# Hand-over of memory between layer 0, the dilation and layer 1, tile by tile, and another order of batches in layer 1

## The chip, the cores and the metric

One core of one Trainium2 chip runs the whole program. The metric is the device time of one execution in microseconds; lower is better. A kernel is timed in several executions and the median is compared. One more execution, taken with the hardware profiler, gives the trace that the numbers below come from.

## What is computed

The reference is a stack of four graph layers over 16 graphs (B = 16) of 1024 nodes (N = 1024) with 128 features, each layer followed by a residual and a layer norm:

```python
x = _layernorm(x + _L0_gnn_ref(x, adj, ...))      # attention over neighbours, then a gate
x = _layernorm(x + _L1_gnn_ref(x, adj, nodemask, ...))
x = _layernorm(x + _L2_gnn_ref(x, adj, ...))      # attention, then three gates
x = _layernorm(x + _L3_gnn_ref(x, adj, ...))      # two graph convolutions
```

Layer 1 first thins the graph out ("dilation") and then runs three SAGE steps over it, with a batch norm over all graphs between them:

```python
def step(carry, n):                    # lax.scan over the 1024 rows, one after the other
    row = jnp.take(carry, n, axis=0); num = jnp.sum(row)
    sf = jnp.where(num > T_DIL, (num + K_DIL - 1) // K_DIL, 1)
    rm = row & (jnp.cumsum(row) % sf == 0)        # and only where the node is valid
    keep = ~rm
    carry = carry.at[n].set(row & keep)
    carry = carry.at[:, n].set(carry[:, n] & keep)
...
out = (einsum('bij,bjd->bid', adj_d, x) / deg) @ Wr + x @ Wx + b    # _sage, then relu and _bn
```

The thinned adjacency of a graph is the "state" of a batch: 1024 x 1024 values in fp8, 8 KB in each of the 128 partitions, 1 MB in all.

## The kernel before

The whole program is unrolled, and a list scheduler of the compiler fixes the order of instructions on every engine ahead of time. It goes by its own estimate of when each instruction can start: where an engine would be free, it takes the first ready instruction in the order of the source. [...] DMAs are issued by SyncE (SP) and by GpSimd (POOL).

On-chip memory is handed out in pools. A pool that is opened where closed pools lay has to wait for their tiles. A pool may do so in two ways: by default ("pool") the first use of any of its tiles waits until all tiles of the older pools below it are free, the last DMA out of them included; with `reuse_waits="tile"` a tile waits only for the older tiles that it lies on. Layers 2 and 3 have the second form already. A pool lays out its buffers in the order in which the source first names them.

- `Yq` (lines 857 to 862) holds the states of all 16 batches: 64 KB on the left side of SBUF for batches 0 to 7, 64 KB on the right side for batches 8 to 15.
- Layer 0 (lines 867 to 980): for each batch `before` (line 888) loads eight slices of the adjacency (`an`, line 895), makes `ab` and `chk` of them and writes the state `Y[b]` (line 905); `attention` (line 930) runs eight steps of score matmul (line 723), masked maximum (`em`, line 942), exponential and weighted sum (line 953); `after` (line 956) gates, normalises (line 772, with the power on GpSimd at line 744) and stores the batch to `x1_d` (line 977). Three batches are in work at a time: `before` of one, `attention` of the one ahead of it, `after` of the one ahead of that.
- The dilation (lines 990 to 1166) goes in 16 steps: 8 column blocks k times two groups g of 8 batches. `prepare` (line 1016) gathers the counts of a block, `fixed_point` (line 1066) finds the removed entries in six evaluations (line 1082), one after the other, and `removal` (line 1118) takes them out of the state of each batch: row sums (line 1128), `q` (line 1130), `keep` (line 1132), the new state (lines 1133 and 1142). In step i the fixed point of step i runs beside the removals of step i-1 and the preparation of step i+1. The two preparations at the start (line 1159) have nothing beside them. Before these stand the lines 999 to 1008: the check value `nomem`, and `dinv`, the power -1/2 of all degrees, on GpSimd (line 1003), turned and sent to DRAM; it is read in layer 3 only.
- In the last column block the states of batches 8 to 15 also go to DRAM (`dil8_d`, line 1144).
- Layer 1 (lines 1222 to 1454) has three steps over all batches in the order 0 to 15. `first` (line 1337) makes the degrees by a matmul (line 1246), brings them back as a broadcast `rdeg` by three small DMAs, splits x in two float32r parts `hi` and `lo` (lines 1236 and 1237), widens the state to float32r (`a`, lines 1256 and 1258) and multiplies (line 1269); `out` (line 1364) applies the weights, `keep` (line 1393) does the next product. Batches 0 to 7 use their state where it lies. The right side is closed on entry and becomes the pool `l1_wide` for `a` (8 buffers) and for `A8` (4 buffers), into which the states of batches 8 to 15 are loaded back.

[...] Layer 0 uses 0 to 3 for the scores (two buffers of two banks), 4 and 5 for `acc`, 6 and 7 for `ph`/`pt`. The dilation before has the row sums `s` in 0 to 2, `pc` in 3 and 4, `s0` in 5 and 6, `pd` in 7.

## Time and profile before

| what | value |
|---|---|
| median of 8 runs | 3125.91 us (3105.04 to 3132.64) |
| the profiled execution's own time | 3121.4 us |
| its span, first to last instruction | 3119.7 us |
| mean granted TensorE clock | 0.966 |
| busy: TensorE, VectorE, ScalarE, GpSimd | 92%, 75%, 65%, 10% of the span |
| layer 0 | up to about 767 us |
| dilation | about 767 to 1184 us |
| layer 1 | about 1184 to 1900 us; layers 2 and 3 from there to the end |

Times inside the execution are counted from the span's first instruction. In the lines of the timeline the first number is the start, the second the duration, then engine, source line, operation, output and inputs; the bracket at the end says how long the engine was idle before it and what ended this. Every table by windows gives for each stretch its length and the busy time of each engine with the number of instructions.

### The profile page before, as it was taken

To read this page: it belongs to the slowest core of one execution; us is meant where nothing else is said; L and a number is where in the kernel's file an instruction comes from. 1 tells how busy PE (TensorE), PEld (TensorE's weight loads), DVE (VectorE), ACT (ScalarE), POOL (GpSimd) and SP (SyncE) were. 2 spreads that over 40 slices of the span, in tenths; PEclk is the share of its full clock that TensorE was granted. 3 is DMA by queue.
4 is the path that set the end of the run, shared out by engine and by line. 5 is a ranking of instruction groups with operands and counts; after the bars stand their busy time and mean duration, and the time that the engine had idled before them with its cause. 6 is when DMAs were issued, how large, how long until landed. Compare 5 with 4: busy or idle time off the path is not lost.

```text
span 3119.7 us, 43208 instructions
## 1 busy us (share of the span) xinstructions
PE 2857.0 (92%) x15442; PEld 1841.0 (59%) x15442; DVE 2331.4 (75%) x5971; ACT 2016.3 (65%) x3393; POOL 327.1 (10%) x292
## 2 busy tenths in 40 slices
PE   7999999996899998999999987999999999989996
PEld 4455555453566655777788874555555555555554
DVE  7888888886899984666678785766767776666665
ACT  5777777774688875655555534766666666666653
POOL 0000000003000001111122231000010010100000
PEclk9999999997999999999999998999999999999997
DMA  5344334440000006223366792011112211111000
GB/s 169 124 148 149 133 131 142 142 135 29 2 2 2 2 6 226 86 82 122 125 214 227 247 325 107 34 55 54 62 67 66 68 64 54 55 55 54 21 14 22
DMA packets 123216, 297.98 MB, mean 96 GB/s; under 512 B 12656, under 2 KB 64624, under 8 KB 115824
## 3 DMA queue, kind: packets, MB, share of 16 engines
q1 hardware_dynamic: 102384, 211.13, 20.6%
q0 software_dynamic: 20608, 84.00, 7.1%
q8 instruction: 124, 2.03, 0.3%
q14 instruction: 100, 0.82, 0.1%
HBM read 211.04 MB, written 84.02 MB: 95 GB/s over the span
## 4 chain that ended last, share of the span: by engine, by line
PE 57%; DVE 22%; issue 5%; ACT 5%; POOL 4%; DMA 2%; POOLq 0%; SPq 0%; DVEq 0%; ACTq 0%
PE acc L1269 9%; PE ph L1510 7%; PE pmm L723 7%; PE acc L1573 5%; PE acc L953 4%; PE ph L765 4%; PE ph L758 4%; PE ph L1373 3%; PE s L1128 3%; POOL ln_rstd L744 3%; DVE ln_st L777 2%; PE ph L1496 2%; DVE mid L1082 2%; PE acc L1246 1%; DVE keep L1132 1%
## 5 line engine op out<-in xcount | busy, mean ns | idle before, releaser
L723 PE MATMUL pmm<-G,hT 128*128 128x512 f32 x1024 | 504.0, 614 | 6.8 <-DVE mx L942 3.5
L723 PEld LDWEIGHTS pmm<-G,hT 128*128 128x128 f32 x1024 | 183.3, 195 | 179.0 <-issue 135.1
L784 ACT ACTIVATE xn<-xn,ln_nb,ln_rstd 128x128 f32<-128x128 f32 x512 | 209.1, 481 | 121.4 <-DVE ln_nb L782 121.3
L1573 PE MATMUL acc<-em,hs 128*128 128x512 f32 x512 | 247.8, 599 | 22.1 <-DVE hs L1570 20.5
L953 PE MATMUL acc<-em,hs 128*128 128x512 f32 x512 | 253.4, 620 | 11.3 <-DVE hs L950 7.9
L744 POOL TENSOR_TENSOR ln_rstd<-ln_rstd,mhalf 128x8 f32<-128x8 f32 x64 | 117.1, 1829 | 1373.9 <-DVE ln_rstd L741 1075.2
L1269 PE MATMUL acc<-a,lo 128*128 128x512 f32 x768 | 241.1, 398 | 1.9 <-DVE lo L1237 1.9
L1269 PE MATMUL acc<-a,hi 128*128 128x512 f32 x768 | 242.0, 399 | 0.9 <-ACT a L1258 0.7
L1128 PE MATMUL s<-step,carry 128*128 128x512 bf16 (+2 forms) x1088 | 212.8, 309 | 3.5 <-DVE carry L1098 3.2
L1130 ACT ACTIVATE q<-s,negc 128x512 f16<-128x512 f32 x256 | 170.6, 694 | 66.8 <-issue 29.3
L1559 DVE CUSTOM_DVE_ANT_0 em<-pmm,msk 128x1024 f32<-128x1024 f32 x128 | 155.7, 1216 | 57.5 <-PE pmm L723 36.4
L1142 ACT ACTIVATE carry<-pc,negone 128x512 fp8e4<-128x512 f32 x256 | 166.7, 695 | 39.7 <-PE pc L1141 29.7
L939 ACT ACTIVATE msk<-carry,l0nbig 128x1024 bf16<-128x1024 fp8e4 x128 | 145.3, 1141 | 62.4 <-DVE mx L942 47.4
L897 ACT ACTIVATE ab<-an 128x1024 bf16<-128x1024 f32 x128 | 134.6, 1052 | 69.6 <-PE pt L904 42.8
L900 DVE SCALAR_TENSOR_TENSOR chk<-an 128x1024 fp8e4<-128x1024 f32 x128 | 156.1, 1219 | 31.3 <-DMA an<-in_adj 30.2
L942 DVE CUSTOM_DVE_ANT_0 em<-pmm,msk 128x1024 f32<-128x1024 f32 x128 | 155.4, 1214 | 27.1 <-PE acc L953 19.3
L1269 PEld LDWEIGHTS acc<-a,lo 128*128 128x128 f32 x768 | 142.8, 188 | 42.8 <-DVE lo L1237 9.5
L953 PEld LDWEIGHTS acc<-em,hs 128*128 128x128 f32 x512 | 93.6, 196 | 123.0 <-issue 95.5
L1554 ACT ACTIVATE msk<-A,nbig 128x1024 bf16<-128x1024 fp8e4 x128 | 145.5, 1138 | 31.0 <-DVE mx L1559 28.7
L905 DVE TENSOR_SCALAR carry<-pt 128x1024 fp8e4<-128x1024 bf16 x128 | 155.1, 1216 | 13.2 <-PE pt L904 12.6
L1573 PEld LDWEIGHTS acc<-em,hs 128*128 128x128 f32 x512 | 92.6, 190 | 117.5 <-issue 79.8
L1269 PEld LDWEIGHTS acc<-a,hi 128*128 128x128 f32 x768 | 141.6, 188 | 33.8 <-ACT a L1258 1.3
(278 smaller groups left out, 6592.3 us busy)
## 6 DMA issues: line engine op xcount, KB each, us to landing
an<-in_adj SPq DMA_DIRECT2D x128, 512.0 KB, 3.4
adj_d<-carry POOLq DMA_DIRECT2D x16, 1024.0 KB, 4.9
A<-dil_d SPq DMA_DIRECT2D x16, 1024.0 KB, 6.3
rdeg<-rdeg_d SPq DMA_DIRECT2D x32, 512.0 KB, 4.2
ag_d<-ag POOLq DMA_DIRECT2D x32, 512.0 KB, 5.4
ag<-ag_d SPq DMA_DIRECT2D x32, 512.0 KB, 6.2
A<-adj_d SPq DMA_DIRECT2D x16, 1024.0 KB, 4.8
xn<-in_x SPq DMA_DIRECT2D x16, 512.0 KB, 3.8
```

Source lines behind the costliest of these rows:

```text
L723: nc.tensor.matmul(p[:, h * 512:(h + 1) * 512], lhsT, rhs[:, h * 512:(h + 1) * 512], start=True, stop=True)
L744: nc.gpsimd.tensor_tensor(r, r, mhalf[:, :n], op=OP.pow)
L784: nc.scalar.activation(r[:, i, :], r[:, i, :], AF.Identity, scale=rstd[:, i:i + 1], bias=nb[:, i:i + 1])
L900: nc.vector.scalar_tensor_tensor(chk, an, 0.0, an, op0=OP.is_gt, op1=OP.not_equal, accum_out=other[:, c:c + 1], saturate=False)
L953: nc.tensor.matmul(s.acc[:, c], hs, em[:, c], start=(jt == 0), stop=(jt == NT - 1))
L1128: nc.tensor.matmul(s[:, lo or 0:], y, twos if lo is None else step[:, :512 - lo], start=(j == 0), stop=(j == len(terms) - 1))
L1130: nc.scalar.activation(q[:, h * 512:(h + 1) * 512], s, AF.Abs, bias=st.negc[:, i:i + 1])
L1142: nc.scalar.activation(Y[b][:, hb, ks], pc, AF.Relu, bias=negone, saturate=False)
L1269: nc.tensor.matmul(acc, part[:, jt, :], pieces[h * NT // 2 + i][:, j, :], start=(jt == 0 and p == 0), stop=(jt == NT - 1 and p == 1))
L1510: nc.tensor.matmul(p, part[:, jt, :], A[:, jt, c], start=(jt == 0 and i == 0), stop=(jt == NT - 1 and i == 1))
L1559: nc.vector.tensor_tensor_reduce(em, e, msk, 1.0, 0.0, op0=OP.add, op1=OP.max, accum_out=mx)
L1573: nc.tensor.matmul(s.acc[:, c], hs, em[:, c], start=(jt == 0), stop=(jt == NT - 1))
```

## The change

1. All pools of layer 0, of the dilation and of layer 1 get `reuse_waits="tile"`.
2. `an`, `ab`, `chk` and `xT` of layer 0 (17,408 bytes in a partition) move to a pool `early` of their own, which is opened first and so lies lowest.
3. The dilation opens its PSUM pools in another order: `s0` gets banks 0 and 1, `pd` bank 2, `s` banks 3 to 5, `pc` banks 6 and 7.
4. The lines 999 to 1008 (check value, power, transposition, store of `dinv`) move behind the two first preparations.
5. The states of batches 0 to 7 lie on the right side and go to DRAM; those of 8 to 15 lie on the left. Layer 1 takes the batches in the order 8 to 15, 0 to 7, in all three steps.

```diff
-    for ctx_, side in ((carry_ctx, "left"), (carry2_ctx, "right")):
+    for ctx_, side in ((carry2_ctx, "right"), (carry_ctx, "left")):
...
-        wts = ph.enter_context(tc.tile_pool(name="l0_w", bufs=1))
...
+        early = ph.enter_context(tc.tile_pool(name="l0_early", bufs=1, reuse_waits="tile"))
+        wts = ph.enter_context(tc.tile_pool(name="l0_w", bufs=1, reuse_waits="tile"))
+        ps_w = ph.enter_context(tc.tile_pool(name="l0_pw", bufs=2, space=PSUM, reuse_waits="tile"))
+        ps_a = ph.enter_context(tc.tile_pool(name="l0_pa", bufs=1, space=PSUM, reuse_waits="tile"))
+        ps_h = ph.enter_context(tc.tile_pool(name="l0_ph", bufs=2, space=PSUM, reuse_waits="tile"))
...
+        work = ph.enter_context(tc.tile_pool(name="l0_work", bufs=1, reuse_waits="tile"))
+        small = ph.enter_context(tc.tile_pool(name="l0_small", bufs=2, reuse_waits="tile"))
...
-                an = work.tile([P, N], F32, name="an", bufs=2)
+                an = early.tile([P, N], F32, name="an", bufs=2)
...
-                ab = work.tile([P, N], BF16, name="ab", bufs=2)
+                ab = early.tile([P, N], BF16, name="ab", bufs=2)
...
-                chk = work.tile([P, N], FP8, name="chk")
+                chk = early.tile([P, N], FP8, name="chk")
...
-                    xT = work.tile([P, N], F32, name="xT")
+                    xT = early.tile([P, N], F32, name="xT")
...
     with ExitStack() as ph:
...
+        sb = ph.enter_context(tc.tile_pool(name="dl_sb", bufs=2, reuse_waits="tile"))
+        small = ph.enter_context(tc.tile_pool(name="dl_small", bufs=3, reuse_waits="tile"))
+        ps_b = ph.enter_context(tc.tile_pool(name="dl_pb", bufs=2, space=PSUM, reuse_waits="tile"))
+        ps_d = ph.enter_context(tc.tile_pool(name="dl_pd", bufs=1, space=PSUM, reuse_waits="tile"))
+        ps_s = ph.enter_context(tc.tile_pool(name="dl_ps", bufs=3, space=PSUM, reuse_waits="tile"))
+        ps_c = ph.enter_context(tc.tile_pool(name="dl_pc", bufs=2, space=PSUM, reuse_waits="tile"))
...
-            if k == NT - 1 and b >= B // 2:
+            if k == NT - 1 and b < B // 2:
                 nc.gpsimd.dma_start(dil8_d[b], Y[b].bitcast(F32))
...
         for s in steps[:G2]:
             for _ in prepare(*s):
                 pass
+
+        nc.vector.tensor_scalar(mx0, mx0, -1.0e15, None, op0=OP.is_lt)
+        nc.vector.tensor_reduce(nomem, mx0, AX.X, OP.max)
+
+        nc.vector.tensor_scalar(deg, deg, 1.0, 1.0, op0=OP.add, op1=OP.max)
+        nc.gpsimd.tensor_tensor(dinv, deg, mhalf[:, 0:1].to_broadcast([P, BT]), op=OP.pow)
+        pt = ps_s.tile([BT, P], F32, name="pt", tag="s")
+        nc.tensor.transpose(pt, dinv, identf)
+        dt = sb.tile([BT, P], F32, name="dt", bufs=1)
+        nc.vector.tensor_copy(dt, pt)
+        nc.sync.dma_start(dinv_d, dt)
...
-        wts = ph.enter_context(tc.tile_pool(name="l1_w", bufs=1))
-        work = ph.enter_context(tc.tile_pool(name="l1_work", bufs=2))
+        wts = ph.enter_context(tc.tile_pool(name="l1_w", bufs=1, reuse_waits="tile"))
+        work = ph.enter_context(tc.tile_pool(name="l1_work", bufs=2, reuse_waits="tile"))
         carry2_ctx.close()
...
+        small = ph.enter_context(tc.tile_pool(name="l1_small", bufs=2, reuse_waits="tile"))
+        ps_h = ph.enter_context(tc.tile_pool(name="l1_ph", bufs=4, space=PSUM, reuse_waits="tile"))
+        ps_a = ph.enter_context(tc.tile_pool(name="l1_pa", bufs=4, space=PSUM, reuse_waits="tile"))
...
-                    if b >= B // 2:
+                    if b < B // 2:
                         st.A = wide_pool.tile([P, NT, N], FP8, name="A8", bufs=4)
...
+        order = [*range(B // 2, B), *range(B // 2)]
...
-            take_turns([step.load(b) for b in range(1 + lead)])
+            take_turns([step.load(b) for b in order[:1 + lead]])
...
-            outs = [step.out(b) for b in range(B)]
+            outs = [step.out(b) for b in order]
...
-                    streams.append(step.load(i + 1 + lead))
+                    streams.append(step.load(order[i + 1 + lead]))
...
-                    streams.append(step.keep(i - 1 - lag[l]))
+                    streams.append(step.keep(order[i - 1 - lag[l]]))
```

## The prediction

> **What bounds the kernel now.** I read the page first: TensorE is busy for 92% of the span, and its row of forty slices dips at the ninth to tenth and at the fifteenth to sixteenth, the two hand-overs that the change is about. Then the busy times by window around them (length; busy time of each engine; granted clock, DMA share and GB/s at the end):

> ```profile
> 700.00:740.00 40.00, 39.65 (x144) 19.84 (x142) 30.38 (x84) 27.90 (x43) 22.95 (x3) 1.00 0.10 40
> 746.60:767.00 20.40, 7.06 (x88) 6.70 (x88) 6.68 (x26) 4.50 (x10) 2.59 (x2) 0.55 0.09 27
> 767.00:777.20 10.20, 2.66 (x64) 2.50 (x64) 10.20 (x41) 0.00 (x0) 0.00 (x0) 0.50 0.02 7
> 777.20:800.00 22.80, 12.17 (x128) 7.29 (x128) 18.38 (x48) 5.89 (x10) 0.00 (x0) 0.65 0.00 1
> 1164.00:1184.00 20.00, 17.52 (x139) 9.89 (x138) 9.28 (x16) 18.74 (x32) 3.79 (x7) 1.00 0.74 301
> 1184.00:1197.00 13.00, 3.53 (x17) 1.42 (x15) 0.00 (x0) 1.23 (x3) 1.06 (x2) 0.82 0.84 285
> 1197.00:1203.70 6.70, 6.13 (x24) 4.92 (x24) 4.38 (x9) 5.23 (x8) 0.19 (x1) 0.59 0.75 214
> 1203.70:1229.70 26.00, 25.29 (x125) 18.08 (x125) 15.43 (x27) 15.89 (x19) 3.44 (x4) 1.00 0.53 193
> ```

> TensorE, full until 740, does 7.1 us of work in the 20.4 us after the last attention product (746.6) and is cold until 800; VectorE, full from 767 to 777, is idle for two thirds before. In layer 1's first 13 us nearly everything stands still. The chain of waits says what ends the first gap:

> ```profile
> 757.54 1.66 POOL ln_rstd L744
> 759.20 3.70 issue
> 762.92 3.86 DMA x_d<-xn
> 766.90 0.29 DVE dt L1007
> ```

> and the timeline what stands in front of what:

> ```profile
> 711.79 20.75 POOL L1003 TENSOR_TENSOR deg<-deg,mhalf 128x128 f32<-128x128 f32 x1 [0.87 <-DVE deg L1002]
> 735.76 0.17 DVE L782 SCALAR_TENSOR_TENSOR ln_nb<-ln_mv,ln_rstd 128x8 f32<-128x8 f32 x1 [0.45 <-POOL ln_rstd L744]
> 766.90 0.29 DVE L1007 COPY dt<-pt 128x128 f32<-128x128 f32 x1 [7.50 <-DMA x_d<-xn]
> 1183.20 0.33 SPq L702 DMA_DIRECT2D Wr<-in_L_gnn_Wr  x1
> 1188.47 6.62 SPq L1319 DMA_DIRECT2D n<-x_d  x3
> 1196.92 1.05 ACT L1236 CAST hi<-n 128x1024 fp32r<-128x1024 f32 x1 [8.79 <-DMA n<-x_d]
> ```

> `dt` has nothing to do with the store of batch 15, yet waits for it: the pool wait. VectorE then holds all of `prepare` behind it. Layer 1's first load is issued when the last removal ends (1183.2), behind five small loads, among the last stores of states (DMA share 0.84), and lands at 1196.9.

> [...] line 1033 follows 0.2 us after `dt`, though its state was ready at 710. [...] the trace has 3.86 us for 512 KB and that is used.

> **Part by part.**

> *Start.* Now the first `an` is issued at 7.69, after the transposed weights (line 816, 6.96 + 0.28) free the raw pool below `work`. `early` lies on nothing old, so it can go after the six small loads (last 3.14 + 0.47): 3.6. ScalarE starts at 12.61 now. Worth 7.69 - 3.6 = 4.1; VectorE is at constants until 7.4, before the data would land (about 8.5), so little is lost: 3.5 us, between 0 (if `xn`, which still lies on the raw weights, stands ahead on SP) and 4.1. Layer 0 is a full TensorE pipeline, so this moves the rest.

> *Layer 0 to dilation.* By the sizes, `sk` (4096 bytes), `front` (6144), `uY` (1024), `dt` (512), `mid` (2048) and half of `q` lie on `early`, whose last readers end at about 708. `s0` waits for the score bank last used by step 6 of the last attention (739.5), `pd` for step 7 (742.3). What then has to run on VectorE from 742.5 on to the first `keep` (794.9 now):
> - the rest of `after`: 6.7 us (746.6:767 row);
> - the second part of `prepare`, 4 times `sk` 0.6 and five small ones, 1.3 each: 5.2 us. The `front`/`uY` part, 4 x (2 x 0.6 + 0.2) = 5.6 us, is ready at 708 and fits the 9.6 us in which VectorE is idle between 700 and 740;
> - six evaluations at 2.1 us (777.17 to 789.4): 12.6 us, with 0.5 us free in each;
> - 5.5 us from the last evaluation to `keep` as now (789.4 to 794.9).
> Sum 30.0, of which about 1 us falls into the free half microseconds: 742.5 + 29 = 771.5, say 773 with imperfect order. `keep` (bytes 17,920 to 19,968 of the pool) lies past `early` and the weights (18,592 together) on the `xn` buffer of batch 15, so it needs the store landed at 766.8: not later. Gain 794.9 - 773 = 22 us.

> *The power moved.* Line 1002 now fills VectorE's first free place after the degrees (711.4) and the 20.75 us power ends at 732.5, just before batch 14's `ln_rstd` (ready 733.9). Behind the preparations in the source, it lets nine ready pieces go first (8 of 0.6 and one or two of 0.2, 5.2 us); the free places after 711.4 are 2.0, 0.9, 1.3, 1.1 us, so it comes at about 722. The power then ends near 743 and batch 14's norm comes at 744.5 instead of 735.8. All of VectorE's list stands behind line 782, attention of batch 15 included. That the order foresees this is unlikely: line 782 waits for the power in all 64 places, 65.4 us in all, so the scheduler holds GpSimd's power for shorter than it is. Cost 744.5 - 735.8 = 9 us. It is nothing if line 1002 stays before 713 or falls just after 735.8; at most 13, if it comes at 750 and holds up batch 15's norm (759.2) instead. I take 9: gain here 22 - 9 = 13.

> *The step loop of the dilation.* Same work. PSUM banks and buffers are as many. Nothing taken; a step lasts 24.7 us on average (line 1102: 789.7 to 1159.6 in 15), single ones 19.1 to 29.6, so an order of another phase could cost or save some: -2 to +2.5 us a step is the bound I give for the range's ends.

> *Dilation to layer 1.* Stores of states move from group 1 (1168 to 1184) to group 0, a step earlier, under removals; GpSimd has nothing else there. The right side is free before the end, so widening (8 pieces, 0.69 or 1.05 us) and the reloads of `A8` can start early. The weights lie on `sk`, free at 1160 or earlier. The first `n` lies on the `front` buffer of the last step, read to about 1180: load at 1180, landing at 1184 (4.0 us, the median of line 1319), then `hi` 1.05 and `lo` 1.22: product at 1187 instead of 1203.7. That is not the gain, since TensorE has work that now comes before: from 1184 to 1203.7 it is busy 3.5 + 6.1 = 9.7 us, idle 10.0, and idle 0.7 up to 1229.7, where the even rhythm of 24.0 us a batch begins. So 10.7 us, plus up to 2.5 us if the degree matmuls (3.6) use TensorE's idle time in 1164:1184, less waits for `n`: 11, between 6 (ScalarE, 18.7 of 20 us busy in the tail, is slowed by widening) and 15. `rdeg` needs about 12 us from the degrees (2.4 + 1.4 + 2.3 + 4.2, and queues), so at 1198, when the first half product is done at 1195: late by 3 us at most while the second half runs.

> *Order of batches.* Eight resident then eight loaded, as now; the same number of everything. 0. Layer 2 begins with batch 0, whose last product is then written five batches before its load: 0.

> Sum: 3.5 + 13 + 11 = 27.5 us of the profiled 3121.4, 3094; the median shown stands 4.5 above that execution: 3098.

> **Rivals.**
> 1. The power does not collide (or moves to a harmless place): 3.5 + 22 + 11 = 36.5, 3089. For it: the second is only one place in a list. Against: the window without loss is 2 us wide.
> 2. The gaps move instead of going: the first `keep` comes behind a late store (power at 750, +13, and one exchange more), layer 1 still waits for `n`: 3.5 + 6 + 4 = 13.5, 3112. For it: both hand-overs keep a tile on a late buffer (`xn`, `front`).
> 3. Slower: the earlier start gives the step loop another interleaving, fixed points standing behind removals in VectorE's list. VectorE is over 90% busy there (36.6 and 37.7 us in the 40 us windows from 800), so misplaced waits add up. At 2.5 us a step, 16 x 2.5 = 40 against 27.5 gained: 3138. It decides above 1.7 us a step. Against it: the loop's code and buffers are the same.
> 4. No change that shows: the same loss at 1.2 us a step, 19 us: 3118. A measurement of this kernel can tell 0.3%, 9 us, from nothing.

> The change could also fail to do what it says, if tiles happen to lie on late buffers; that is rival 2.

> **Numbers.** Forecast 0.44, rival 1 0.26, rival 2 0.17, rival 3 0.06, no change 0.07. Faster by over 0.3%: 0.44 + 0.26 + 0.17 = 0.87; within 0.07; slower 0.06. The range runs from rival 1 with its best ends (start 4, first hand-over 26, second 15: 45 us, 3080) to just past rival 2: 3113. Left out are the last two cases and a little beyond 3080, under 2 in 10.

> **What would show it.** Right: first `an` issued before 4; `dt` no longer waiting for a store; line 1051 before 750; first `keep` at 770 to 785 minus the start's gain; the 20.75 us power between 715 and 745 with line 782 idle for several us behind it; the time from the last removal to the even rhythm down from 46 to about 35 us; mean step 24.7. Wrong: line 782 waiting 1 us or less (rival 1); `keep` or `hi` still waiting on a store or load for over 5 us (rival 2); steps of 26 us and more (rivals 3, 4).

## The result and the profile after

The changed kernel takes 3100.33 us in the median (11 runs, 3085.49 to 3106.89); the kernel before took 3122.61 us beside it (32 runs, 3102.62 to 3134.26). The ratio is 0.993 with a 95% interval of 0.991 to 0.9949, so 16 to 28 us were gained. The profiled execution has a time of 3097.59 us of its own and a span of 3095.9, 23.8 less than before, at the same mean clock of 0.966.

From the page of the changed kernel, the busy tenths of TensorE and its clock in forty slices:

```profile
PE   7999999996999989999999988999999999999995
PEclk9999999998999999999999998999999999999997
```

The sixteenth slice, where layer 1 begins, is a 9 now (before, an 8); the 8 in the fifteenth lies inside the dilation. In the tenth the busy digit is 6 as before, with the clock at 8 instead of 7, and the eleventh went from 8 to 9. The same stretches as before, by windows (length; busy time of PE, weight loads, VectorE, ScalarE, GpSimd; clock, DMA share, GB/s): the last `after`, the preparations, the fixed points up to the first `keep`, and the start of layer 1.

```profile
737.40:751.70 14.30, 6.50 (x78) 4.95 (x77) 6.66 (x26) 1.32 (x2) 1.66 (x1) 0.77 0.01 3
751.70:761.90 10.20, 2.62 (x64) 2.47 (x63) 10.20 (x41) 3.18 (x8) 0.93 (x1) 0.50 0.18 52
761.90:785.00 23.10, 12.71 (x128) 7.51 (x128) 18.43 (x49) 5.94 (x10) 0.00 (x0) 0.63 0.01 4
1166.60:1171.50 4.90, 4.16 (x24) 2.49 (x22) 1.15 (x1) 4.83 (x8) 0.53 (x1) 1.00 1.13 362
1171.50:1197.50 26.00, 25.94 (x137) 19.13 (x137) 16.75 (x30) 14.94 (x19) 3.74 (x4) 1.00 0.25 74
```

The 20.4 us in which VectorE did 6.7 us of work have become 14.3 us with the same 6.7: the wait for the store is gone. But the 10.2 us in which VectorE does nothing but prepare are still there, still behind `after`. In front of layer 1, 45.7 us (1184.0 to 1229.7) have become 30.9 (1166.6 to 1197.5), with TensorE busy for 30.1 of them. The timeline of the changed kernel shows the same instructions as before:

```profile
7.63 1.23 DVE L902 SCALAR_TENSOR_TENSOR chk<-an 128x1024 fp8e4<-128x1024 f32 x1 [1.45 <-DMA an<-in_adj]
705.00 20.75 POOL L1157 TENSOR_TENSOR deg<-deg,mhalf 128x128 f32<-128x128 f32 x1 [0.87 <-DVE deg L1156]
734.11 0.68 PE L1041 MATMUL s<-step,carry 128*128 128x128 bf16 x17
751.67 0.17 DVE L782 SCALAR_TENSOR_TENSOR ln_nb<-ln_mv,ln_rstd 128x8 f32<-128x8 f32 x1 [1.85 <-POOL ln_rstd L744]
751.75 0.28 DVE L1023 TENSOR_TENSOR uY<-carry,upper 128x128 int32<-128x128 int32 x1
761.26 0.28 DVE L1161 COPY dt<-pt 128x128 f32<-128x128 f32 x1
779.93 0.75 DVE L1122 TENSOR_SCALAR keep<-q,wid 128x1024 fp8e4<-128x1024 f16 x1
1160.89 4.25 SPq L1321 DMA_DIRECT2D n<-x_d  x3
1169.28 1.04 ACT L1238 CAST hi<-n 128x1024 fp32r<-128x1024 f32 x1
```

The first `keep` of the kernel before, for comparison:

```profile
794.91 0.75 DVE L1132 TENSOR_SCALAR keep<-q,wid 128x1024 fp8e4<-128x1024 f16 x1
```

The first `chk` starts at 7.63 instead of 12.64. The power has kept its place in the order: it still follows straight on the degrees. TensorE does the first column sums of the dilation at 734, inside layer 0. VectorE's first piece of prepare, `uY`, comes 0.08 us behind line 782 of batch 15, without waiting for anything. `n` is loaded 5.7 us ahead of the end of the last removal (1166.6), not after it.

The chain of waits, which before went from `ln_rstd` over 3.86 us of DMA to `dt`, now goes from `ln_rstd` (749.97) over line 782 straight on into prepare.

Four marks cut each trace into stretches: the issue of layer 0's last store, the first `keep`, the end of the last removal, and the third power of layer 1 (the first of its rhythm of 24.0 us). A fifth mark stands for the start of layer 2: the end of its first long interval between powers, within which its first batch already runs. The last three columns are explained below. All numbers are us, and each row is one trace; the rows under the first two belong to the experiments.

| trace | last store | to first `keep` | to end of last removal | to third power | layer 2 start to end | lost to half clock | rest |
|---|---|---|---|---|---|---|---|
| before | 762.92 | 31.99 | 388.94 | 77.80 | 1128.1 | 42.1 | 1086.0 |
| changed | 755.35 | 24.58 | 386.65 | 62.91 | 1135.7 | 50.8 | 1084.9 |
| before_again | 761.30 | 32.08 | 385.44 | 78.15 | 1145.7 | 62.5 | 1083.2 |
| after_again | 753.34 | 24.60 | 385.75 | 63.61 | 1145.1 | 62.5 | 1082.6 |
| start_only | 758.71 | 32.04 | 388.99 | 77.66 | 1138.3 | 54.0 | 1084.3 |
| first_two | 759.58 | 24.57 | 386.41 | 78.86 | 1148.4 | 65.8 | 1082.6 |
| second_only | 761.67 | 32.05 | 384.55 | 64.46 | 1134.6 | 50.4 | 1084.2 |
| order_back | 755.80 | 24.58 | 386.35 | 74.60 | 1121.1 | 35.1 | 1086.0 |
| gates_before | 761.42 | 32.06 | 384.48 | 77.42 | 1140.5 | 33.3 | 1107.2 |
| gates_after | 758.50 | 24.60 | 386.70 | 63.38 | 1139.3 | 31.5 | 1107.8 |
| prep_early | 769.59 | 13.16 | 385.88 | 62.25 | 1149.2 | 66.2 | 1082.9 |
| prep_power | 759.35 | 15.57 | 387.05 | 62.24 | 1145.3 | 60.9 | 1084.4 |
| best | 759.49 | 16.08 | 387.81 | 62.24 | 1138.8 | 31.3 | 1107.5 |
| wide_best | 762.81 | 15.49 | 386.85 | 62.31 | 1125.6 | 35.2 | 1090.4 |

At the third power the changed kernel was 32.2 us ahead (1229.49 against 1261.65), at the end only 23.8. Of the missing 8.4 us, 7.6 lie behind the start of layer 2 (1135.7 against 1128.1). Three windows each hold one batch there; first two of the kernel before, then one of the changed kernel:

```profile
2476.85:2548.48 71.63, 66.64 (x267) 40.62 (x266) 50.62 (x155) 47.88 (x93) 6.75 (x4) 1.00 0.18 59
2620.45:2695.41 74.96, 69.97 (x266) 42.84 (x266) 50.63 (x154) 48.20 (x94) 6.75 (x4) 0.96 0.17 57
```

```profile
2371.14:2446.10 74.96, 69.97 (x266) 42.84 (x266) 50.63 (x154) 48.20 (x94) 6.75 (x4) 0.96 0.17 56
```

The work of VectorE and GpSimd is the same to 0.01 us and that of ScalarE to 0.3; TensorE's took 3.3 us longer, at a clock of 0.96. Finer windows, again of the kernel before, show where. The first window is the run of 32 gate matmuls of three columns (lines 1583 and 1584) in the quick batch, the second what follows after 2.4 us of the same run in a slow one:

```profile
2545.20:2548.70 3.50, 3.50 (x33) 3.49 (x32) 3.50 (x20) 1.78 (x3) 0.00 (x0) 1.00 0.24 42
2694.20:2700.90 6.70, 6.70 (x20) 4.63 (x21) 1.55 (x7) 4.85 (x11) 1.77 (x2) 0.50 0.45 157
```

In a slow batch the clock drops to one half inside that run and stays there for 6.7 us, which costs 3.35. The column "lost to half clock" is the sum of (1 - clock) times the length over windows of 1 us from the start of layer 2 on. Before it is 42.1, changed 50.8: the difference of 8.7 covers the 7.6. The rest is the same to 1.1 us. Some 19 us of the loss stand in the last 80 us of both traces, so they are no part of the difference.

### The profile page after: what moved, and what is told of

It is laid out like the page before. It is cut to its first block, busy times and chain, and to the rows that moved or that the text cites. A ratio compares the mean times of both kernels' runs of the same rounds, so it can differ in the third digit from the quotient of the medians.

```text
span 3095.9 us, 43185 instructions
## 1 busy us (share of the span) xinstructions
PE 2852.0 (92%) x15442; PEld 1840.8 (59%) x15442; DVE 2331.4 (75%) x5971; ACT 2016.7 (65%) x3393; POOL 327.2 (11%) x292
## 4 chain that ended last, share of the span: by engine, by line
PE 58%; DVE 21%; ACT 5%; issue 4%; POOL 4%; DMA 2%; SPq 0%; POOLq 0%; ACTq 0%; DVEq 0%
PE acc L1271 9%; PE ph L1514 7%; PE pmm L723 7%; PE acc L1577 5%; PE acc L955 4%; PE ph L765 4%; PE ph L758 4%; PE ph L1375 4%; POOL ln_rstd L744 3%; PE s L1118 2%; DVE ln_st L777 2%; PE ph L1500 2%; DVE mid L1072 2%; PE acc L1248 2%; DVE keep L1122 1%
## 5 line engine op out<-in xcount | busy, mean ns | idle before, releaser
L744 POOL TENSOR_TENSOR ln_rstd<-ln_rstd,mhalf 128x8 f32<-128x8 f32 x64 | 117.1, 1829 | 1382.5 <-DVE ln_rstd L741 1063.0
L1120 ACT ACTIVATE q<-s,negc 128x512 f16<-128x512 f32 x256 | 170.4, 696 | 58.0 <-DVE negc L1099 22.3
L1563 DVE CUSTOM_DVE_ANT_0 em<-pmm,msk 128x1024 f32<-128x1024 f32 x128 | 155.7, 1216 | 65.4 <-PE pmm L723 43.1
L907 DVE TENSOR_SCALAR carry<-pt 128x1024 fp8e4<-128x1024 bf16 x128 | 155.0, 1217 | 13.5 <-PE pt L906 13.3
```

The lines of the kernel that those rows point to most:

```text
L744: nc.gpsimd.tensor_tensor(r, r, mhalf[:, :n], op=OP.pow)
L1120: nc.scalar.activation(q[:, h * 512:(h + 1) * 512], s, AF.Abs, bias=st.negc[:, i:i + 1])
L1563: nc.vector.tensor_tensor_reduce(em, e, msk, 1.0, 0.0, op0=OP.add, op1=OP.max, accum_out=mx)
```

## The experiments

### start_only, first_two, second_only, order_back: the parts by themselves

start_only, the kernel before with this alone (the weight, PSUM and small pools of layer 0, and `ab`, `chk` and `xT`, alike):

```diff
+        early = ph.enter_context(tc.tile_pool(name="l0_early", bufs=1, reuse_waits="tile"))
-        work = ph.enter_context(tc.tile_pool(name="l0_work", bufs=1))
+        work = ph.enter_context(tc.tile_pool(name="l0_work", bufs=1, reuse_waits="tile"))
...
-                an = work.tile([P, N], F32, name="an", bufs=2)
+                an = early.tile([P, N], F32, name="an", bufs=2)
```

> The kernel before with parts 1 and 2 of the change for layer 0 alone (pool `early`, tile waits of layer 0's pools). Marks in the traces so far, before and after: store of batch 15 issued at 762.92 and 755.35; first `keep` 794.9 and 779.93; third power of layer 1 (the first of its even rhythm of 24.0 us) 1261.65 and 1229.49. Theory: the earlier start is worth 6.7 us by itself and is carried through unchanged, since the waits behind it are still those of whole pools: store at 756, first `keep` at 788, third power at 1255. Rival 1, the size I predicted: 3.5 us (759.4, 791.4, 1258). Rival 2: what is won at the start is lost again at the hand-over because `keep` waits for something else: `keep` still at 794 or later.

Store 758.71, `keep` 790.75, third power 1257.40: 4.2 us earlier than before at all three. What the start wins is carried through, so rival 2 falls; the size lies nearer to rival 1 (3.5) than to the 6.7 that the theory had taken from one pair of traces. The end of this trace was 2.7 us later than before, with 11.9 us more lost to half clock. (It is one trace.)

first_two, the changed kernel with:

```diff
-        order = [*range(B // 2, B), *range(B // 2)]
+        order = [*range(B)]
...
-        work = ph.enter_context(tc.tile_pool(name="l1_work", bufs=2, reuse_waits="tile"))
+        work = ph.enter_context(tc.tile_pool(name="l1_work", bufs=2))
```

(sides, stores of states and the other pools of layer 1 likewise)

> The changed kernel without part 5 and without the tile waits of layer 1: start and first hand-over alone. Theory (the gains are separate sums): first `keep` at 780 as in the changed kernel, third power of layer 1 at 1261.65 - 6.7 - 8.2 - 2.4 = 1244.4, where 2.4 is what the last three steps of the dilation ran shorter. Rival: the first hand-over is only worth something together with the second (the time goes into a longer wait in front of layer 1): third power at 1250 or later. In both the end moves by less than this if layer 2 again gives some of it back: in the changed kernel 32.2 us were won at the third power and 23.8 at the end.

`keep` 24.57 us after the store, as in the changed kernel; the third power at 1249.4, 5 us later than the sum had it, 4.2 of them because layer 0 ended at 759.58 and not at 755.35 (start_only and gates_after, with the same code for layer 0, have 758.71 and 758.50). It lies only 0.6 us below the rival's limit of 1250, but the stretches tell the two apart: from the last removal to the third power it takes 78.9 us, about as before (77.8 and 78.1), so at most 1 us of the 7.5 went into a longer wait there. So the first hand-over is worth 7.5 us without the second. The median was 3112.13 us beside 3115.05 for the kernel before, ratio 0.9969 (0.9948 to 0.999), that is 3 to 16 us, with 65.8 us lost to half clock in the trace.

second_only, the kernel before with part 5 and `reuse_waits="tile"` in the pools of layer 1.

> The kernel before with part 5 and the tile waits of layer 1: second hand-over alone. Theory: last removal as before at 1183.9, first `n` load issued about 6 us ahead of it (1178), third power at 1261.65 - 14.9 = 1246.8. Rival: part of the 14.9 us needed the earlier dilation (stores of states landing earlier, removals in another phase): third power at 1250 to 1255. Where the end stands depends on the clock in layer 2: 0 to 10 us less than the gain at the third power.

First `n` at 1172.58, 5.7 us ahead of the end of the last removal at 1178.27, as in the changed kernel. From there to the third power 64.46 us, 13.3 less than before. Little of the second hand-over hangs on the first. Median 3105.78 us beside the same 3115.05, ratio 0.9966 (0.9943 to 0.999), that is 3 to 18 us. The stretches put 12.4 us on the first two parts and 13 to 15 on this one; the medians agree with both, but their intervals are too wide to tell them apart.

order_back, the changed kernel with the sides, the stores and the order of batches of before.

```diff
-        order = [*range(B // 2, B), *range(B // 2)]
+        order = [*range(B)]
...
-            if k == NT - 1 and b < B // 2:
+            if k == NT - 1 and b >= B // 2:
```

> The changed kernel with the sides, the stores of states and the order of batches of before (part 5 undone, all tile waits kept). Theory: the pieces `a` of layer 1 and the reloaded states lie on the states of batches 8 to 15, which are taken last by the removals and then stored, so the first `a` waits for stores that are issued up to the last removal and take 6 to 8 us (the last of before: issued at 1184 to land at about 1191): the third power comes 8 to 15 us later than in the changed kernel, 1238 to 1244; the tile waits of layer 1 are worth little without part 5. Rival: the tile waits alone do it, the order is worth nothing: 1229.5, within 2 us.

74.60 us to the third power: the tile waits alone give 3.2 us, part 5 on top of them gives the other 11.7, as the theory had it in size (one trace). Part 5 without the tile waits of layer 1 was not run. The theory's reason is not what the trace shows first. The timeline of order_back behind the last removal:

```profile
1178.78 1.05 ACT L1238 CAST hi<-n 128x1024 fp32r<-128x1024 f32 x1 [6.81 <-DMA n<-x_d]
1180.68 0.29 DVE L1296 TENSOR_TENSOR ws<-Wr,Wx 128x128 f32<-128x128 f32 x1 [8.41 <-DMA Wx<-in_L_gnn_Wx]
```

and its table of DMA issues between 1120 and 1190 (KB each, median us from issue to landing), then that of the changed kernel:

```profile
n<-x_d SPq DMA_DIRECT2D x3, 512.0 KB, 13.9
```

```profile
n<-x_d SPq DMA_DIRECT2D x4, 512.0 KB, 5.5
```

With the old order the eight stores of states (1 MB each) are issued from 1151 to 1167, beside the loads that layer 1 starts with; in the changed kernel the last is issued at 1147. `n` takes 13.9 us instead of 5.5; SyncE is held for 7.24 us at the issue of `Wr` (1168.11), so that Wx is issued only at 1175.39 and lands at 1180.7; and the first `a` stands behind the sum `ws` of the weights on VectorE. That the stores are what slows the loads is inferred from these times. Whether `a` would have waited for the stores as well can't be seen behind this.

### after_again, before_again: is the loss in layer 2 the kernel's?

> The changed kernel once more, unchanged. If which batches of layer 2 lose clock is chance of phase, the list of their lengths differs from the first trace (four of 71.6, then 75 to 77) although nothing else does, and so does the end; the third power of layer 1 stays within 3 us of 1229.5. If it belongs to the kernel, the list is the same again.

> The kernel before once more, for a second trace of it. Theory (the clock's loss in layers 2 and 3 is chance): from the start of layer 2 to the end the time without the loss is 1083 to 1086 us as in seven other traces, with the loss anything from 1121 to 1149; the lengths of the batches differ from the first trace (seven of 71.6, then 75 to 77). The last store of layer 0 comes at 761 to 763, the first `keep` 32.0 after it, the third power of layer 1 77 to 79 after the last removal. Rival (the loss belongs to the kernel): the same list again, 1128.

Neither list came back, so the kernel is not what decides which batches are slow. Behind the first interval, the changed kernel went on with 73.3, 74.9, 77.1, 73.3 us instead of four times 71.6 and lost 62.5 us to half clock instead of 50.8; the kernel before went on with 71.6, 74.9, 77.1, 73.3 instead of seven times 71.6 and lost 62.5 instead of 42.1. ("Phase" in the expectations is where a batch lies against the step between the clock's drops, which the last section estimates; that it decides which batches are slow was my estimate, and these traces do not show it.) The third power came at 1227.30 and 1256.97, within 5 us of the first traces. Over the ten traces with the unchanged layer 2, layers 2 and 3 took 1121 to 1149 us with the loss and 1082.6 to 1086.0 without. The 8.4 us that were given back in the profiled execution are not a price of the change. They are not needed for the median's 22 us either: what the parts are worth by their stretches is added up below. The second series gave 3100.17 us, ratio 0.9917 (0.9886 to 0.9947).

### gates_before, gates_after: splitting the run of small matmuls

The half of the gates that reads `xT` is computed in `before` and kept in `gx`, so that `after` has 16 of the matmuls and not 32.

```diff
             for p, c in products(ps_h, (W2T, s.xT)):
                 nc.scalar.activation(s.hT[:, c], p, AF.Identity, bias=b2)
+            pg = ps_h.tile([P, NT, 3], F32, name="pg", tag="h")
+            for i in range(NT):
+                nc.tensor.matmul(pg[:, i, :], s.xT[:, i * P:(i + 1) * P], gw[:, 0, :], start=True, stop=True)
+            s.gx = small.tile([P, NT, 3], F32, name="gx")
+            nc.vector.tensor_add(s.gx, pg, gb[:, None, :].to_broadcast([P, NT, 3]))
...
-                nc.tensor.matmul(pg[:, i, :], s.xT[:, c], gw[:, 0, :], start=True, stop=False)
-                nc.tensor.matmul(pg[:, i, :], hpT[:, c], gw[:, 1, :], start=False, stop=True)
+                nc.tensor.matmul(pg[:, i, :], hpT[:, c], gw[:, 1, :], start=True, stop=True)
...
-            nc.vector.tensor_add(gt, pg, gb[:, None, :].to_broadcast([P, NT, 3]))
+            nc.vector.tensor_add(gt, pg, s.gx)
```

> The kernel before with one edit in layer 2: the half of the three gates that reads xT is computed in `before` and kept, so that the run of 32 matmuls of three columns in `after` (3.6 us of TensorE) becomes two runs of 16 at different places; one addition of 0.17 us more per batch. The theory on the rest of the time: in the six traces so far the granted TensorE clock falls to 0.5 for 6.8 us inside this run in some batches of layer 2 and not in others (71.6 us a batch against 75 to 77), a loss of 17 us in layer 2 before, 27 after and 40 in the kernel with the first two parts. [...] Then splitting the run ends the loss: 71.6 us in every batch, the end 17 us earlier (3105), and the runs scatter less than the 37 us of before. Rival: the clock falls for a budget of work or power that builds up over the kernel; then it falls at another place in the same batches and the time stays near 3115 to 3122.

> The changed kernel with the same edit in layer 2. If the clock's loss in layer 2 is of phase and ends with the edit, the changed kernel gains more by it than the kernel before (27 against 17 us in the traces at hand): 3070, and the difference between the two kernels with the edit is what the hand-overs are worth: start 5 (3.3 to 7.6 in four traces), first 7.5, second 14.9, 27 in all. Rival (budget of work or power): the difference stays at 8 to 24 us, since what is won earlier is paid back later.

The expected times failed: 3132.47 us (22 runs, 3121.96 to 3137.87) and 3109.22 (6 runs, 3104.18 to 3111.83), both later than without the edit. The batches of layer 2 became regular, 73.3 to 74.6 us in both kernels, and the runs scatter over 16 and 8 us (22 and 6 runs) where the kernel before scattered over 38 beside them (27 runs). The loss went down (33.3 and 31.5 us), but the time without it rose to 1107 to 1108 us, 1.4 a batch, and eight of the first twelve intervals still lose some:

```profile
2280.40:2284.20 3.80, 3.78 (x20) 3.35 (x19) 2.61 (x6) 2.41 (x6) 0.00 (x0) 0.56 0.00 0
```

This window of gates_after follows a gap of 2.9 us in which TensorE waits for `ehi` (the kernel before waits for it for 2.92 us at 2807.57). So the clock falls at another place, which is what the rival had said, and the edit is no improvement. What stands ahead of each drop tells more. Two windows of the kernel before, each of 3.41 us (the step estimated from the times of the drops in the last section) and each ending where the clock drops in layer 2:

```profile
2690.76:2694.17 3.41, 3.41 (x28) 2.93 (x26) 3.41 (x20) 2.75 (x3) 0.00 (x0) 1.00 0.10 32
2803.40:2806.81 3.41, 1.25 (x3) 0.19 (x1) 3.33 (x6) 3.41 (x9) 0.00 (x0) 1.00 0.00 0
```

The first is busy throughout, with 23 of the small matmuls in it; in the second TensorE stands idle for most of the time. From the start of layer 2 on, each of the ten traces with the gates as they were has 6 to 14 drops of the first sort (3.3 us of work or more, 21 to 30 small matmuls in the 3.41 us ahead), and 5 to 8 of the second. In the four traces with the gates split or turned round (gates_before, gates_after, best, wide_best) there is none of the first sort: the 3.41 us ahead of every drop hold at most 2.61 us of work. This speaks against a budget of work or power that builds up over the kernel, which would not go with the run: in these fourteen traces the first sort stands at the run of 32 small matmuls alone. Why the clock drops there is not shown. The edit also made the comparison cleaner: the two kernels with it differ by 23.5 us in the mean (21.0 to 26.2, from resampling the runs).

### prep_early, prep_power: why prepare stands behind layer 0

```diff
+            if k == 0:
+                pair = early.tile([P, N], F32, name="an", bufs=2)
+                st.sk = pair[:, :N // 2].bitcast(F16).rearrange("p (b j) -> p b j", j=P)
+                st.front = pair[:, N // 2:].bitcast(BF16).rearrange("p (b j) -> p b j", j=P)
+            else:
+                st.sk = sb.tile([P, GB, P], F16, name="sk")
...
-            st.v1m = small.tile([P, GB], F32, name="v1m")
+            st.v1m = (small if k else kept).tile([P, GB], F32, name="v1m")
```

(`uY` on `ab`, `mid` on `chk`, `l1`, `ti` and `thr` on the small pool `kept`, all for k = 0; `early` and `kept` stay open to the end of the dilation)

> The changed kernel, with the tiles of the two first preparations and of the first two fixed points (sk, front, uY, mid, v1m, l1, ti, thr of column block 0) taken from pools that stay open: `an`, `ab` and `chk` of `early` are used once more, and a small pool is opened before layer 0. The addresses are as free as before, only the pool is an open one. Theory: in the changed kernel VectorE's list has the whole preparation behind line 782 of batch 15 (751.75), though nothing in it waits, because the order of instructions hands out tiles of a newly opened pool on VectorE only behind layer 0's last instruction there. Then here uY and front come before 715, sk at 737 to 744, one evaluation before line 782; five evaluations of 2.1 and 5.5 us to `keep`: the first `keep` 13 to 14 us after the last store is issued, against 24.6 now: 11 us gained. And what I predicted of the power should now come true: line 1156 falls behind eight pieces of 0.2 to 0.7 us, the 20.75 us power ends at about 735 and line 782 of batch 14 waits for 4 to 9 us; net 2 to 7 us. Rival: VectorE's list is ordered so for another reason (its own estimate of VectorE being full): no piece of prepare before 750 and `keep` 24.6 us after the store.

Both halves came true, but not the 2 to 7 us that were to be left over. `sk` was written before line 782 of batch 15, and `keep` came 13.16 us after the store instead of 24.58. And the power, now behind eight pieces of prepare, came at 716.80, where all other traces have it between 702.7 and 711.8. GpSimd and VectorE in prep_early:

```profile
716.80 21.06 POOL L1173 TENSOR_TENSOR deg<-deg,mhalf 128x128 f32<-128x128 f32 x1 [11.19 <-DVE deg L1172]
```

```profile
739.52 0.17 DVE L782 SCALAR_TENSOR_TENSOR ln_nb<-ln_mv,ln_rstd 128x8 f32<-128x8 f32 x1 [9.53 <-POOL ln_rstd L744]
```

VectorE stood still for 9.53 us in front of line 782 of batch 14, the last store came at 769.59, 6.7 us later than in any other trace, and the gain was gone (third power 1230.88 against 1229.49).

prep_power puts the lines of part 4 back ahead of the two preparations:

> The two first preparations in open pools, with the lines of the power put back ahead of them, and the gates of layer 2 as they were. In the trace with both edits and split gates the first `keep` came 7.5 us earlier than with split gates alone, and the end 10.7. Theory: the same 7.5 to 10.7 us against the changed kernel, 3090 to 3093 of 3100; `keep` 16 us after the last store is issued. Rival: the gain is eaten, as in prep_early: 3100.

```profile
708.18 22.67 POOL L1006 TENSOR_TENSOR deg<-deg,mhalf 128x128 f32<-128x128 f32 x1 [0.88 <-DVE deg L1005]
```

```profile
733.68 0.17 DVE L782 SCALAR_TENSOR_TENSOR ln_nb<-ln_mv,ln_rstd 128x8 f32<-128x8 f32 x1 [1.56 <-POOL ln_rstd L744]
```

Line 782 waits for 1.56 us, `keep` comes 15.57 after the store, 9.0 us less than in the changed kernel. The median is 3087.14 us (3071.99 to 3094.96), ratio 0.9873 (0.9836 to 0.991) to before, and 11.4 us (1.4 to 21.1) less in the mean than after_again, timed beside it. With wide_best below it is the fastest of these kernels. It undoes part 4, so with open pools part 4 is not needed; what parts 3 and 4 are worth by themselves in the changed kernel was not run.

### best, wide_best: with layer 2 changed as well

best is prep_power with the split gates.

> prep_early with the lines of the check value and the power put back ahead of the two preparations (undoing part 4), and with the edit of the gates. Theory: the power starts right after the degrees (about 705) and delays nothing, so the 11 us of the first hand-over stay whole; layer 1's first n, which lies on tiles that nobody uses after the first column block, is not late either. Against gates_after: 11 us less, about 3059. Rival: the fixed point that starts earlier ends up waiting for the last store (`keep` behind x_d): 3 to 5 us less.

3098.63 us, 10.5 less in the mean than gates_after (7.7 to 13.3), as expected in the difference and not in the level; `keep` 16.08 us after the store.

wide_best is prep_power with the gates the other way round (the gate vectors and `xT`, `hpT` have changed places in the matmul; the 32 old matmuls are gone):

```diff
+            for p, c, _ in halves(ps_h):
+                nc.tensor.matmul(p[:3], gw[:, 0, :], s.xT[:, c], start=True, stop=False)
+                nc.tensor.matmul(p[:3], gw[:, 1, :], hpT[:, c], start=False, stop=True)
+                nc.scalar.copy(gs[:, c], p[:3])
...
+                nc.tensor.transpose(pg[:, i, :], gs[:, i * P:(i + 1) * P], identf[:3, :3])
```

> prep_power with the gates of layer 2 computed the other way round: four matmuls of 512 columns with the three gate vectors as the stationary side, a copy of 3 x 1024 values by ScalarE, and eight transpositions of three columns, in place of the 32 matmuls of three columns. The split cost 1.4 us a batch of its own and moved the clock's loss to a gap of 2.9 us elsewhere; here the small matmuls shrink from 3.6 to about 0.9 us[...]. Theory of the phase: the clock no longer falls at the gates, a batch of layer 2 takes 71.6 us or 1 us less, and the end is 20 to 35 us earlier than that of prep_power: 3055 to 3070. Rival 1: the longer way from PE over ScalarE to PE stands on the path of `after`, as the split did: batches of 73 us and more, no gain. Rival 2: a budget: the loss comes back at another place, 3090.

```profile
2203.00:2345.00 142.00, 133.15 (x494) 75.29 (x493) 99.10 (x305) 96.15 (x187) 13.76 (x8) 1.00 0.18 60
```

Two batches at a clock of 1.00; of the twelve intervals eight are 71.6 or 71.8 us, four 73 to 74. The theory held for the clock: the loss at the gates is gone. The time did not follow: 3088.93 us, 2.3 us (-5.3 to 10.1) off prep_power. That is rival 2's number (3090), but the loss did not come back: it is 35.2 us against 60.9. In the traces layers 2 and 3 became 19.7 us shorter (1125.6 against 1145.3): 25.7 less lost, 6.0 more without the loss. But from the third power of layer 1 to the start of layer 2 it took 735.7 us instead of 723.0, and layer 0 ended 3.5 later. This stretch already holds the first batch of layer 2 with its edited gates (its interval is 71.9 us against 68.6), and all four kernels with edited gates have 732.7 to 736.1 us there; 723.0 is the shortest of the ten others (to 730.7). How much of the 12.7 us is the edit and how much scatter is not shown.

## Why the prediction was right, and which of its steps were not

The forecast of 3098 us for the median and 3094 for the profiled execution met 3100.33 and 3097.59. The sum behind it, 27.5 us, came close because two steps failed in opposite senses and two terms were too small; that these made up for one another is luck.

*Start, 3.5.* Right mechanism, too small a term. The first `an` was issued at 3.65 as predicted, but it took 4.0 us to land instead of 4.95, and VectorE's list now has the rest of its constants behind the first `chk` (`identb` at 8.78), not ahead of it: the first `chk` came 5.0 us earlier. The six traces with the changed layer 0 and nothing else in it have their last store at 753.3 to 759.6, mean 756.9; the four with the old one (the split gates included) at 761.3 to 762.9, mean 761.8: 4.9 us. The scatter of one trace is as large as the term; the 7.6 us of the first pair is not its size.

*Layer 0 to dilation, 22.* The step that failed is "the `front`/`uY` part is ready at 708 and fits the 9.6 us in which VectorE is idle", and with it the evaluations beginning during `after`. It was free of the store, and the stretch from the store to `keep` lost 7.4 us (7.5 in the mean of all traces that have it), as long as `dt` had waited. But VectorE's list kept all of prepare behind line 782 of batch 15. prep_early shows that the tiles' pool decides this: in pools that stay open the same pieces move up, and this stretch is 11.4 us shorter again (in that trace the late power takes it back, in prep_power 9.0 are kept). That the order of instructions gives out tiles of a newly opened pool only behind the older ones' last work on VectorE is inferred from this; PSUM tiles did move up (line 1041 at 734). The term measured 7.5, and `keep` at 779.93 still fell within the 770 to 785 less the start's gain that was named as a sign. (TensorE's clock is not low until 800 in the trace before: it is back at 1.00 at 792.95. The sum did not use this.)

*The power moved, -9.* It did not collide: line 1157 ran at 705.00, and line 782 of batch 14 waited for 0.45 us as before. The reason is the same failed step: the nine pieces that were to go before line 1156 were not there to go. Where they were, in prep_early, the power came 11.8 us later than in the changed kernel (about 10 was predicted) and line 782 waited for 9.53 us. So 13 was predicted for the two steps together, by two errors of 14.5 and 9, and 7.5 was measured. The sign of the first rival, line 782 waiting for 1 us or less, is the one that came; its 3089 would have needed the 22 as well.

*Step loop, 0.* Right: 24.5 us a step (line 1092: 774.60 to 1142.10), and 385.8 to 386.7 from `keep` to the last removal against 385.4 and 388.9. The 2.3 us between the first two traces go with the clock: over all fourteen traces this stretch is 384.5 us where less than 0.1 is lost to half clock, 386.3 to 387.1 where 3.4 are, and 388.9 to 389.0 where 6.8 are.

*Dilation to layer 1, 11 between 6 and 15.* Right mechanism: `n` issued 5.7 us ahead of the end of the last removal (3.9 predicted), the first product 3.8 behind it (3.2 predicted). The term was too small: 14.5 in the mean of three pairs of traces (77.8 to 63.3; that with the split gates is one of them). I had counted TensorE's idle time, 10.7 us, and taken its busy time as work, except for up to 2.5 us of degree matmuls that could move ahead. From the last removal to the third power, with the part of it that ran at half clock, before, and then changed:

```profile
1183.85:1261.65 77.80, 67.00 (x349) 50.45 (x349) 42.47 (x72) 41.16 (x54) 10.12 (x14) 0.93 0.48 166
1192.30:1202.56 10.26, 5.52 (x22) 4.67 (x22) 3.23 (x7) 4.17 (x6) 0.00 (x0) 0.50 0.77 204
```

```profile
1166.58:1229.49 62.91, 62.11 (x344) 47.61 (x342) 40.24 (x68) 38.84 (x51) 9.71 (x14) 1.00 0.31 101
```

Idle time went from 10.8 to 0.8 us, busy time from 67.0 to 62.1. Of these 4.9 us, 2.8 are half clock (half of the 5.52 us that TensorE was busy at 0.50; the rest of the 10.26 us it stood idle, and that is counted already), and about 1.4 are 5 of the 64 degree matmuls, which now run ahead of the end of the last removal. Together 14.2 of the 14.9 us of this pair; 0.7 stay open.

*Order of batches, 0.* As a step by itself wrong: without it the second hand-over is worth 3.2 us, not 14.5, with the stores of states beside layer 1's first loads. The prediction had put those stores under the second hand-over, so the sum was not touched.

So the parts are worth 4.9 + 7.5 + 14.5 = 26.9 us. The medians say 22.3 (16 to 28) and, for the pair with regular batches, 23.5 (21.0 to 26.2); the sum lies a little outside the second interval, and where the 3 us go is not shown. What the prediction did not have is the term of layer 2: 35 to 66 us lost to half clock in layers 2 and 3 of a program whose remaining layers it took to be only moved along. Of this, 15 to 39 us stand at the run of small matmuls and differ from execution to execution of one kernel; the rest stands at gaps, some 19 us of it in the last 80 us of every trace with the gates as they were.

## What to carry to other kernels

A tile that is free by address isn't early by that alone: look whether its instructions have moved up in their engine's list, and if not, whether a pool that stays open moves them; and when they do, look at what they are now in front of. When a gap of TensorE is to be closed, count a clock below 1 as lost time beside idle time, but only where TensorE is busy; where it stands idle, the time is counted already. And before a difference of some 0.3% is explained, split the trace at marks and compare each stretch between several executions of the same kernel.

## What the runs showed of the hardware

The power of 128 x 128 values on GpSimd lasts 20.75 us (before, changed), and 21.06 us in prep_early and 22.67 in prep_power, where VectorE does pieces of prepare beside it; the reason was not looked for.
